# Differential attention's last batch beside the experts, and its q and k weights folded into one matrix

## The chip, the cores and the metric

The kernel runs on one core of a Trainium2 chip. The metric is the device time of one execution in microseconds. Three runs of the kernel before took 1086.4 to 1087.47 us, median 1086.97. A separate execution was taken with the hardware profiler; all profile lines below come from that one. TensorE is called PE here, VectorE DVE, ScalarE ACT, GpSimd POOL and SyncE SP. All data are float32.

## What is computed

The program is two transformer blocks on an input of 8 batches x 512 tokens x 128 channels. Block 0 adds, to x, a 16-head causal attention (head size 8) and a soft mixture of experts, both of the normalised x. Block 1 adds two things to the new x:

```python
# differential attention, per batch of 512 tokens, no mask, D = 128
q1, q2 = split(xn @ w_q12);  k1, k2 = split(xn @ w_k12);  v = xn @ w_v
diff = softmax(q1 @ k1.T * D**-0.25) - lam * softmax(q2 @ k2.T * D**-0.25)
out  = diff @ v;  out / rms(out) * 0.2

# a layer norm, a causal attention over the batch axis (8 positions), a projection, a second norm,
# then a top-2 router over 8 experts with 1280 slots each
exp_out = gelu(tokens_of_expert @ moe_w1[e]) @ moe_w2[e]
moe[token] += exp_out * prob            # each token appears in two experts
```

Since the score is `xn Wq Wk^T xn^T`, the product `Wq Wk^T` of the two weights is a 128 x 128 matrix that does not depend on the tokens.

## The kernel before, in words

The kernel has four stages, and the change is in the last two.

Stages 1 and 2 (to about 717 us) are block 0 and most of a side chain called *leads*. `l1_load` (L149) loads block 1's weights and `l1_fold` (L177) prepares them, early in stage 1, between two pieces of PE work that go in the order in which they are written. There is one lead for each of the 8 batches: the generator `lead` (L665). It runs block 1's norm, the attention over the batch axis (POOL multiplies, L722 and L751, one product a batch position; DVE sums them, through the helper at L616), the projection, the second norm and the routing, and ends with eight *puts* (L896): indirect DMAs on POOL's queue, 128 rows each, which scatter the tokens into the experts' slots `xs` in DRAM. A lead needs its batch's output of block 0, so the leads of batches 5, 6 and 7 are unfinished when stage 2 ends.

Stage 3 is the *joint stage*. The generator `diff` (L1327) does differential attention for eight batches. For a batch, `diff_qk` (L1243) makes q1, k1, q2, k2, each with a 128x512 matmul and an ACT eviction; `diff_v` makes v; then, for each of four row blocks, `diff_scores` makes two 128x512 score matmuls (L1270), a DVE maximum (L1274) and an ACT exponential (L1275); `diff_both` subtracts the two softmaxes on DVE; `diff_T` transposes; `diff_out` multiplies with v (L1304) and squares on ACT (L1308); after the last row block four small POOL instructions make the scale `ri` (L1313 to L1316), and `diff_end` (L1318) adds the result to `x_all` on DVE and stores the batch as the output's base rows (L1370). The loop at L1377 takes one step of `diff` and then lets `step_leads` (L1162) take at most one step of each unfinished lead. The turn in which a lead may go on depends on what it waits for, and one POOL step is allowed in a turn. `in_order` (L230) then fixes this order on PE, DVE, ACT and POOL.

Stage 4 is the *experts* (L1391). An expert's 1280 slots are loaded with one DMA (`xe`, L1393, after all 64 puts), in three blocks of 4, 4 and 2 tiles of 128 rows. A block is transposed and scaled (L1413), multiplied up (L1421), put through Gelu on ACT (L1424), multiplied down (L1428), scaled on DVE (`es`, L1434) and added to the output rows by indirect DMAs on POOL's queue (L1439), one a tile, ten an expert, eighty in all; these are called *backs*. Two experts may hold the same token, and so an expert's backs wait until all backs of the expert before it have landed. Expert 0's backs wait for the eight base stores. The order in stage 4 is not fixed by `in_order`: the framework's scheduler interleaves it, and it may put DVE instructions of the first experts among the last ones of `diff`.

PSUM in stage 3 is held by pools `d` (3 banks, scores), `o` (2) and `t` (3); in stage 4 by `s` (2 x 2 banks), `o` (2) and `t` (2), which take the same banks over.

Of the kernel before, what the change touches and what calls it, by code (L numbers as in the profile page):

```python
# [25 lines left out]
def kernel(ctx: ExitStack, tc: tile.TileContext, a: dict, out: bass.AP):  # L26
# [122 lines left out]
    def l1_load():  # L149
        for name, key, n in (  # L150
            ("wq1", "L1_attn_w_q12", 2 * D), ("wk1", "L1_attn_w_k12", 2 * D), ("wv1", "L1_attn_w_v", D),
            ("wr", "L1_ffn_router_weight", NE),
        ):
            l1p[name] = const.tile([P, n], F32, name=name)
            nc.sync.dma_start(out=l1p[name], in_=a[key])
        cols = const.tile([P, 4], F32, name="cols")
# [20 lines left out]
    def l1_fold():  # L177
        cols, lam, wnat = l1p["cols"], l1p["lam"], l1p["wnat"]

        lprod = wkb.tile([P, 2, D], F32, name="lprod", bufs=1)  # L180
        nc.gpsimd.tensor_tensor(out=lprod, in0=lam[:, 0:4:2], in1=lam[:, 1:4:2], op=ALU.mult)
# [6 lines left out]
        l1p["nlam"] = nlam  # L188

# [445 lines left out]
    def ln_stats(name, rows):  # L635
        stt = small.tile([P, 4, 6], F32, tag="bn_st", name=f"st_{name}")
        mv = small.tile([P, 4, 2], F32, tag="bn_mv", name=f"mv_{name}")
        for k, r in enumerate(rows):
            dve.bn_stats(out=stt[:, k, :], in_=r)
            dve.bn_aggr(out=mv[:, k, :], in_=stt[:, k, :])  # L640
            yield 1, "dve"
# [23 lines left out]
    def lead(s_):  # L665
# [37 lines left out]
        yield from after("sc", s_ - 1)  # L703
        sc = wt("sc", [NI * H, NB])
# [15 lines left out]
        for t in range(n):  # L720
# [3 lines left out]
            if len(behind) > BEHIND:  # L724
                yield 1, "dve"
                sum_q(*behind.pop(0))
# [22 lines left out]
        for t in range(n):  # L749
# [8 lines left out]
            if len(behind) > BEHIND:  # L758
                yield 1, "dve"
                dve.tensor_tensor(out=at4, in0=at4, in1=behind.pop(0), op=ALU.add)  # L760
# [130 lines left out]
        yield 3, "pool"  # L891

        for i in range(NI):
            m = s_ * NI + i
            for k in range(2):
# [8 lines left out]
                yield 1, "pool"  # L904
# [4 lines left out]
    with ExitStack() as at:  # L909
# [252 lines left out]
        def step_leads(slot_, pe_free, pool_free, more):  # L1162
            room[0] = min(room[0] + more, more)
            spare[0] = min(spare[0] + more * SPARE, CAPA * more)
            for r in list(leads):
                if slot_ < r[1] or (r[2] == "pe" and not pe_free) or (r[2] == "pool" and not pool_free):
                    continue
                if r[2] == "dve" and room[0] <= 0 or r[2] == "act" and spare[0] <= 0:
                    continue
                if r[2] == "pool":  # L1170
                    pool_free = False
                nxt = next(r[0], None)
                if nxt is None:
# [52 lines left out]
    with ExitStack() as l1b:  # L1226
# [9 lines left out]
        wka = l1b.enter_context(tc.tile_pool(name="wka", bufs=2, reuse_waits="tile"))  # L1236


        ascale = D ** (-0.25)
        OUT = (1.0 - LAMBDA_INIT) * math.sqrt(D)  # L1240
        dd = {}

        def diff_qk(b):  # L1243
            for n, (w, c) in enumerate((("wq1", 0), ("wk1", 0), ("wq1", 1), ("wk1", 1))):
                pq = psum_t(f"pqk_{b}_{n}")
                nc.tensor.matmul(pq, lhsT=l1p[w][:, c * D : (c + 1) * D], rhs=xnT[:, b], start=True, stop=True)
                dd["qk", b, n] = o = wka.tile([P, T], F32, tag=f"qk1_{n}", name=f"qk1_{b}_{n}")
                nc.scalar.activation(o, pq, AF.Identity, scale=ascale if w == "wq1" else 1.0)  # L1248
                yield
# [10 lines left out]
        def diff_scores(b, i):  # L1260
# [7 lines left out]
            for k in range(2):  # L1268
                sc = psum_t(f"s1_{u}_{k}", "d")
                nc.tensor.matmul(  # L1270
                    sc, lhsT=dd["qk", b, 2 * k][:, i * P : (i + 1) * P], rhs=dd["qk", b, 2 * k + 1],
                    start=True, stop=True,
# [25 lines left out]
        def diff_out(b, i):  # L1298
            if i == 0:
                dd["po", b] = psum_o(f"po1_{b}")  # L1300
                dd["ss", b] = small.tile([P, NI], F32, tag="ss1", name=f"ss1_{b}")
            po, dT, ss = dd["po", b][:, i * D : (i + 1) * D], dd["dT", b, i], dd["ss", b]
            for c in range(NI):
                nc.tensor.matmul(  # L1304
                    po, lhsT=dT[:, c * P : (c + 1) * P], rhs=dd["v", b][:, c], start=(c == 0), stop=(c == NI - 1),
                )
            junk = wka.tile([P, D], F32, tag="sqj1", name=f"sqj1_{b}_{i}")
# [10 lines left out]
        def diff_end(b):  # L1318
            po, ri = dd["po", b], dd["ri", b]
            for i in range(NI):  # L1320
                nc.vector.scalar_tensor_tensor(
# [3 lines left out]
            store(b)  # L1325

        def diff(bs):  # L1327
# [9 lines left out]
            more = diff_qk(bs[1])  # L1337
# [34 lines left out]

        slot_ = 4 * (N3 + 4)
        tail = len(nc.cur_bb.bb.instructions)
        run = diff(range(NB))
        going = True
        while going or leads:  # L1377
            going = next(run, "end") != "end"
            for _ in range(1):
                step_leads(slot_, True, True, 9.0)  # L1380
                slot_ += 1
        in_order(tail)
# [8 lines left out]
        for e in range(NE):  # L1391
            xe = wk.tile([P, NCT, W], F32, tag="xe", name=f"xe_{e}", bufs=3)
            get = nc.sync.dma_start(out=xe, in_=xs[e * CAP : (e + 1) * CAP].rearrange("(c p) d -> p c d", p=P))  # L1393
            for name in puts:
                tc.add_manual_dep(get.ins, name, sync, reason="any token may be in this expert's slots")

            first = small.tile([P, NCT], F32, tag="first", name=f"first_{e}", bufs=2)
# [8 lines left out]
            es = wk.tile([P, NCT, D], F32, tag="es", name=f"es_{e}", bufs=4)  # L1406
            backs.append([])
            for c0 in range(0, NCT, 4):
                n = min(4, NCT - c0)
                w = n * P  # L1410
                t = transpose4(f"xeT_p{e}_{c0}", [xe[:, c0 + k, :D] for k in range(n)])
                xeT = wk.tile([P, T], F32, tag="xeT", name=f"xeT_{e}_{c0}")
                nc.vector.tensor_scalar(  # L1413
                    out=xeT[:, :w], in0=t[:, :w], scalar1=cols[:, 2:3], scalar2=cols[:, 3:4], op0=ALU.mult, op1=ALU.add
                )
                hT = wk.tile([P, NHC, T], F32, tag="hTm", name=f"hTm_{e}_{c0}")
                for hp in range(NHC // 2):
                    ph = psum_s(f"phm_{e}_{c0}_{hp}")
                    for k in range(2):
                        hc = 2 * hp + k  # L1420
                        nc.tensor.matmul(  # L1421
                            ph[:, k, :w], lhsT=w1_1[:, e, hc * P : (hc + 1) * P], rhs=xeT[:, :w], start=True, stop=True
                        )
# [62 lines left out]
```

## Time and profile before

| | |
|---|---|
| median of three runs | 1086.97 us |
| the profiled execution's own time | 1084.87 us |
| its span, first to last instruction | 1083.1 us |
| PE matmul busy / PE weight load busy | 974.5 us (90%) / 599.0 us (55%) |
| DVE / ACT / POOL busy | 664.2 (61%) / 553.0 (51%) / 565.6 (52%) us |
| joint stage, first q matmul to the end of the last put | 717.6 to 889.0 us |
| first back to last back | 918.08 to 1077.51 us |

A busy share is a mean over four stages with different limits, so it doesn't tell what ends a stage. A line of a timeline gives the start, the time, the engine, the line of the kernel, the operation, out<-in and the count; in brackets stands the idle time of that engine just before, and what ended it by the profile. Where several semaphores are waited for, the one that came last is named, and where the named engine had long been done, it was another. "issue" means that the profile shows nothing that was waited for.

### The profile page before, as it was taken

How to read it: one execution, taken by the hardware profiler on the slowest of the kernel's cores; microseconds unless marked ns; L12 is line 12 of the kernel's file. 1: busy time of each engine (PE TensorE's matmuls, PEld its weight loads, DVE VectorE, ACT ScalarE, POOL GpSimd, SP SyncE). 2: the span in 40 equal slices, each digit the busy share in tenths (PEclk: the TensorE clock that was granted, in tenths of full speed). 3: DMA queues.
4: the chain of work that ended last, by engine and by line, in shares of the span. 5: the costliest groups of instructions: out<-in, count | busy, mean ns of one | idle time of the engine just before them, and what ended most of it. 6: DMA issues, size and time to landing. Idle time of an engine off the chain costs nothing.

```text
span 1083.1 us, 18816 instructions
## 1 busy us (share of the span) xinstructions
PE 974.5 (90%) x6726; PEld 599.0 (55%) x6726; DVE 664.2 (61%) x2126; ACT 553.0 (51%) x1263; POOL 565.6 (52%) x793
## 2 busy tenths in 40 slices
PE   6889899989999999999899999978867987999992
PEld 3457556867545454454444444435545655777772
DVE  6734643277777788888778887258676654222220
ACT  3466348353467576766565656527454653222220
POOL 3201000201242527775878879775867361777776
PEclk8999999999799999999999999779988998999997
DMA  8730000000000000000000000050000013342312
GB/s 252 158 85 2 1 1 1 2 2 1 1 1 2 2 1 2 21 2 2 14 9 3 19 2 21 2 172 1 20 11 20 21 38 103 49 67 38 31 15 25
DMA packets 49310, 32.97 MB, mean 30 GB/s; under 512 B 12232, under 2 KB 44275, under 8 KB 49216
## 3 DMA queue, kind: packets, MB, share of 16 engines
q1 hardware_dynamic: 34832, 24.80, 8.6%
q0 software_dynamic: 13568, 6.70, 4.5%
q8 instruction: 53, 0.87, 0.3%
q14 instruction: 41, 0.34, 0.1%
q10 hardware_dynamic: 816, 0.26, 0.1%
HBM read 17.56 MB, written 17.07 MB: 32 GB/s over the span
## 4 chain that ended last, share of the span: by engine, by line
PE 64%; POOL 14%; DVE 11%; issue 5%; ACT 2%; DMA 2%; POOLq 0%; DVEq 0%; SPq 0%; ACTq 0%
PE se L1068 12%; PE pem L1428 7%; PE phm L1421 6%; PE po L1093 6%; POOL xs L896 4%; PE sm L1035 3%; PE lg_d L302 3%; PE pe L477 3%; PE psl L346 3%; DVE junk L1045 2%; PE pf L379 2%; PE pq L955 2%; PE lg_c L302 2%; PE ph L451 2%; PE s L1270 2%
## 5 line engine op out<-in xcount | busy, mean ns | idle before, releaser
L1045 DVE CUSTOM_DVE_ANT_0 junk<-sm,cmask 128x128 f32<-128x128 f32 (+3 forms) x512 | 249.5, 487 | 69.3 <-PE sm L1035 31.2
L1073 ACT ACTIVATE pt<-se 128x384 f32<-128x384 f32 (+1 forms) x384 | 185.4, 527 | 158.7 <-PE sm L1035 109.7
L1035 PE MATMUL sm<-kj,qT 32*128 32x256 f32 (+3 forms) x1024 | 231.6, 487 | 5.7 <-DVE mcol L1045 3.0
L1068 PE MATMUL se<-q,kj 32*128 32x128 f32 (+3 forms) x1024 | 211.3, 483 | 3.9 <-DVE mcol L1045 3.5
L1439 POOL DMA_INDIRECT out_dram<-es,to x80 | 124.0, 1551 | 46.8 <-issue 22.8
L1068 PEld LDWEIGHTS se<-q,kj 32*128 32x128 f32 x1024 | 99.3, 190 | 84.7 <-DVE mcol L1045 26.1
L1078 POOL TENSOR_SCALAR_AFFINE_SELECT pt<-pt 128x512 f32<-128x512 f32 (+1 forms) x96 | 80.1, 835 | 115.8 <-ACT pt L1073 115.6
L1035 PEld LDWEIGHTS sm<-kj,qT 32*128 32x128 f32 x1024 | 112.6, 191 | 23.8 <-DVE mcol L1045 10.1
L1093 PE MATMUL po<-pt,vpad 128*18 128x512 f32 (+3 forms) x1024 | 91.4, 454 | 12.6 <-POOL pt L1078 12.6
L1424 ACT ACTIVATE hTm<-phm 128x1024 f32<-128x1024 f32 (+1 forms) x48 | 42.2, 881 | 109.2 <-PE phm L1421 109.2
L1428 PEld LDWEIGHTS pem<-w,hTm 128*128 128x128 f32 x640 | 77.1, 192 | 16.8 <-ACT hTm L1424 12.1
L1428 PE MATMUL pem<-w,hTm 128*128 128x128 f32 x640 | 81.2, 278 | 0.5 <-ACT hTm L1424 0.2
L1275 ACT ACTIVATE ex<-s,nm 128x512 f32<-128x512 f32 x64 | 43.9, 687 | 70.3 <-DVE nm L1274 69.7
L1434 DVE TENSOR_SCALAR es<-pem,wt 128x128 f32<-128x128 f32 x80 | 22.9, 345 | 90.0 <-PE pem L1428 90.0
L1421 PE MATMUL phm<-xeT,w 128*128 128x512 f32 (+1 forms) x192 | 75.2, 523 | 2.3 <-DVE xeT L1413 2.3
L896 POOL DMA_INDIRECT xs<-l_z,sput x64 | 65.8, 1028 | 17.0 <-issue 16.0
L508 POOL TENSOR_TENSOR x_all<-x_all,bo_bc 128x512 f32<-128x512 f32 x8 | 10.2, 1275 | 119.4 <-DVE xn L266 119.4
L1270 PE MATMUL s<-qk,qk 128*128 128x512 f32 x128 | 63.9, 620 | 6.6 <-ACT qk L1248 6.4
L1093 PEld LDWEIGHTS po<-pt,vpad 128*18 128x18 f32 x1024 | 20.9, 98 | 64.1 <-POOL pt L1078 24.0
L1274 DVE TENSOR_REDUCE nm<-s 128x1 f32<-128x512 f32 x64 | 42.9, 682 | 9.0 <-PE s L1270 8.6
L1421 PEld LDWEIGHTS phm<-xeT,w 128*128 128x128 f32 x192 | 33.6, 191 | 23.1 <-issue 17.2
L722 POOL TENSOR_TENSOR l_prod<-l_qkv 128x512 f32<-128x512 f32 x36 | 45.6, 1277 | 0.6 <-DVE l_at L616 0.6
(262 smaller groups left out, 1865.4 us busy)
## 6 DMA issues: line engine op xcount, KB each, us to landing
xs<-cmask SPq DMA_DIRECT2D x1, 5280.0 KB, 23.8
xe<-xs SPq DMA_DIRECT2D x8, 660.0 KB, 4.7
x_all<-in_L_attn_x_dram SPq DMA_DIRECT2D x8, 256.0 KB, 4.6
w<-in_L_ffn_w_dram SPq DMA_DIRECT2D x1, 2048.0 KB, 8.8
w<-in_L_ffn_moe_w_dram SPq DMA_DIRECT2D x1, 2048.0 KB, 10.0
out_dram<-x_all SPq DMA_DIRECT2D x8, 256.0 KB, 2.2
out_dram<-es,to POOLq DMA_INDIRECT x80, 3.2
xs<-l_z,sput POOLq DMA_INDIRECT x64, 2.3
```

The lines of the kernel that those rows point to most:

```text
L302: nc.tensor.matmul(lg, lhsT=lhs(k), rhs=rhs, start=True, stop=True)
L896: put = nc.gpsimd.indirect_dma_start(out=xs, out_offset=bass.IndirectOffsetOnAxis(ap=sput[:, k, m : m + 1], axis=0), in_=z2[:, i], in_offs ...
L1035: nc.tensor.matmul(sc[:, o : o + w], lhsT=st["qT", b][rr, i * P : (i + 1) * P], rhs=st["k", b, j][rr, :w], start=True, stop=True,)
L1045: nc.vector.tensor_tensor_reduce(out=junk[:, :w], in0=sc[:, o : o + w], in1=cmask[:, 512 - w : 512], scale=-1.0, scalar=BIG, op0=ALU.add, ...
L1068: nc.tensor.matmul(sc[:, o : o + w], lhsT=st["k", b, j][rr, c * P : (c + 1) * P], rhs=st["q2", b, (g % G) // 2][rr, c * P : T], start=True ...
L1073: nc.scalar.activation(st["pt", g, k][:, r, :o], sc[:, :o], AF.Exp)
L1078: nc.gpsimd.affine_select(out=pt[:, :, :n, :P], in_=pt[:, :, :n, :P], pattern=[[0, 4], [0, n], [1, P]], compare_op=ALU.is_ge, fill=0.0, ba ...
L1093: nc.tensor.matmul(po[32 * r : 32 * r + 2 * PW, c * P : T], lhsT=vpads[b % 3][:, c, at_ : at_ + 2 * PW], rhs=pt[:, r, o : o + w], start=(c ...
L1270: nc.tensor.matmul(sc, lhsT=dd["qk", b, 2 * k][:, i * P : (i + 1) * P], rhs=dd["qk", b, 2 * k + 1], start=True, stop=True,)
L1421: nc.tensor.matmul(ph[:, k, :w], lhsT=w1_1[:, e, hc * P : (hc + 1) * P], rhs=xeT[:, :w], start=True, stop=True)
L1428: nc.tensor.matmul(pe[:, k * D : (k + 1) * D], lhsT=hT[:, hc, k * P : (k + 1) * P], rhs=w2_1[:, e, hc, :], start=(hc == 0), stop=(hc == NH ...
L1439: back = nc.gpsimd.indirect_dma_start(out=out_rows, out_offset=bass.IndirectOffsetOnAxis(ap=to[:, c : c + 1], axis=0), in_=es[:, c], in_of ...
```

## The change

1. `l1_fold` transposes the four 128x128 halves of the q and k weights (PE), evicts them (ACT), multiplies them in two 128x128 matmuls into `wm1` = [Wq1 Wk1^T | Wq2 Wk2^T], and scales on eviction. `diff_qk` then makes two tiles for a batch instead of four, and the scores take `xnT` itself as the moving operand.
2. Batch 7 (`LATE`) is left out of the joint stage, whose loop runs over seven batches. Its base rows are stored without differential attention.
3. The experts are written as a pipeline of 24 blocks: the first half of the next block's up matmuls, half of this block's down matmuls, the other half of the ups, the transposes of the block after next, the other half of the downs. The whole of stages 3 and 4 is now fixed by one `in_order`.
4. From block 6 on (expert 2), three steps of batch 7's `diff` are taken in each block (two after the first half, one after the second), until its twenty-odd steps are done in block 12 (expert 4). Its scores and outputs use the two-bank pool `t`; its exponentials alternate with the Gelus on ACT, which in the built program brings 12 more loads of ACT's function table. Its four small `ri` instructions stand on POOL between the backs of experts 3 and 4.
5. Batch 7's scaled result goes to the output by one accumulating DMA on POOL's queue (`late_add`, 256 KB) between the backs of experts 6 and 7. It waits for all of expert 6's backs, and expert 7's backs wait for it.
6. In `lead`, a batch's first products may start when the lead two before it is through (was: one before; its score tile has two buffers now), and puts have a kind of their own. In a turn a lead that waits to put comes last, and POOL's one step goes to another lead first.

In the built programs the loop takes 152 turns until the last lead is through before and 118 after. On PE the order is the same up to the first matmul of `diff`, but for the six matmuls of the new fold.

```diff
 def l1_fold():
+        wqk = l1p["wqk"]
+        t = transpose4("wqkT_p", [wqk[:, n, c * D : (c + 1) * D] for c in range(2) for n in range(2)])
+        wqkT = wkb.tile([P, NI, D], F32, tag="xn2", name="wqkT", bufs=3)
+        nc.scalar.copy(wqkT.rearrange("p k d -> p (k d)"), t)
+        pm = psum_t("wm1_p")
+        for c in range(2):
+            nc.tensor.matmul(
+                pm[:, c * D : (c + 1) * D], lhsT=wqkT[:, 2 * c], rhs=wqkT[:, 2 * c + 1], start=True, stop=True
+            )
+        l1p["wm"] = wm1 = const.tile([P, 2 * D], F32, name="wm1")
+        nc.scalar.activation(wm1, pm[:, : 2 * D], AF.Identity, scale=D ** (-0.25))
...
 def lead(s_):
-        yield from after("sc", s_ - 1)
-        sc = wt("sc", [NI * H, NB])
+        yield from after("sc", s_ - 2)
+        sc = wt("sc", [NI * H, NB], bufs=2)
...
-        yield 3, "pool"
+        yield 3, "put"
...
-                yield 1, "pool"
+                yield 1, "put"
...
-        def step_leads(slot_, pe_free, pool_free, more):
+        def step_leads(slot_, pe_free, pool_free, more, at_once=()):
-            for r in list(leads):
+            for r in sorted(leads, key=lambda r: bool(at_once) and r[2] == "put"):
...
         def diff_qk(b):
-            for n, (w, c) in enumerate((("wq1", 0), ("wk1", 0), ("wq1", 1), ("wk1", 1))):
...
+            for c in range(2):
+                pq = psum_t(f"pqk_{b}_{c}")
+                nc.tensor.matmul(
+                    pq, lhsT=l1p["wm"][:, c * D : (c + 1) * D], rhs=xnT[:, b], start=True, stop=True
+                )
+                dd["qk", b, c] = o = wka.tile([P, T], F32, tag=f"qk1_{c}", name=f"qk1_{b}_{c}")
+                nc.scalar.copy(o, pq)
                 yield
...
-                sc = psum_t(f"s1_{u}_{k}", "d")
+                sc = psum_t(f"s1_{u}_{k}", "d" if b not in LATE else "t")
                 nc.tensor.matmul(
-                    sc, lhsT=dd["qk", b, 2 * k][:, i * P : (i + 1) * P], rhs=dd["qk", b, 2 * k + 1],
-                    start=True, stop=True,
+                    sc, lhsT=dd["qk", b, k][:, i * P : (i + 1) * P], rhs=xnT[:, b], start=True, stop=True
                 )
...
-        run = diff(range(NB))
+        run = diff(range(LATE[0]))
...
-                step_leads(slot_, True, True, 9.0)
+                step_leads(slot_, True, True, 9.0, ('none',))
-        in_order(tail)
+        for b in LATE:
+            store(b)
...
+        def late_add(e):
+            for _ in late:
+                pass
+            new = []
+            for b in LATE:
+                add = nc.gpsimd.dma_start(
+                    out=out[b].rearrange("(i p) d -> p i d", p=P),
+                    in_=dd["po", b].rearrange("p (i d) -> p i d", i=NI), accum_op=ALU.add,
+                )
+                for name in backs[e + 1]:
+                    tc.add_manual_dep(add.ins, name, sync, reason="a row is read and written by each addition")
+                new.append(add.ins.name)
+            backs[e + 1] = new
+
+        BLOCKS = [(e, c0, min(4, NCT - c0)) for e in range(NE) for c0 in range(0, NCT, 4)]
+        AFTER = 6
...
+        expert_T(*BLOCKS[0])
+        expert_T(*BLOCKS[1])
+        expert_up(*BLOCKS[0], 0)
+        expert_up(*BLOCKS[0], 1)
+        for m, (e, c0, n) in enumerate(BLOCKS):
+            if c0 == 0 and e + 2 < NE:
+                rows_get(e + 2)
+            half = range(n // 2), range(n // 2, n)
+            for hp in range(2):
+                if m + 1 < len(BLOCKS):
+                    expert_up(*BLOCKS[m + 1], hp)
+                if hp == 1 and m + 2 < len(BLOCKS):
+                    if BLOCKS[m + 2][1] == 0:
+                        rows_in(BLOCKS[m + 2][0])
+                    expert_T(*BLOCKS[m + 2])
+                expert_down(e, c0, n, half[hp])
+                late_steps(((2,1)[hp]) if m >= 6 else 0)
+            if e == AFTER and c0 + n == NCT:
+                late_add(e)
+        in_order(tail)
```

`rows_get`, `rows_in`, `expert_T`, `expert_up` and `expert_down` hold the load, the slot columns, the transposes, the up and Gelu, and the down, `es` and backs of the old loop, with the same shapes. `late_steps(n)` takes n steps of batch 7's `diff`.

## The prediction

> **What bounds it now.** I read the page first, then the busy times by stretch, then the timeline of POOL in the last stage, then the timeline around 889 us. The sum below is made against the profiled execution: span 1083.1, own time 1084.87; the median of the runs shown (1086.97) is 3.9 above that span, and I add 3.9 at the end. A difference under 0.2% can't be told from no change.
>
> Busy times of the joint stage (columns: PE, PE weight load, DVE, ACT, POOL, granted clock, DMA share, GB/s), and of two experts:
>
> ```profile
> 717.60:848.00 130.40, 106.29 (x478) 66.86 (x476) 97.85 (x209) 69.92 (x192) 87.99 (x130) 0.93 0.09 26
> 848.00:889.00 41.00, 41.00 (x212) 27.31 (x211) 26.81 (x67) 30.25 (x88) 23.69 (x46) 1.00 0.06 18
> 717.60:889.00 171.40, 147.29 (x687) 94.17 (x686) 124.66 (x274) 100.17 (x280) 111.68 (x176) 0.94 0.08 24
> 980.00:1020.00 40.00, 39.18 (x235) 29.61 (x235) 10.45 (x32) 10.57 (x12) 30.69 (x20) 1.00 0.25 32
> ```
>
> Until 848 no engine is full: the leads' chain from POOL to DVE paces all queues (PE idles 24.1 us). From 848 on PE is. In the experts the chain of waits names PE, and PE looks full, but the end is set elsewhere. Timeline, POOL's backs and the `es` that feed the last expert:
>
> ```profile
> 918.08 1.68 POOL L1439 DMA_INDIRECT out_dram<-es,to  x1 [9.89 <-DVE es L1434]
> ...
> 1053.36 1.13 DVE L1434 TENSOR_SCALAR es<-pem,wt 128x128 f32<-128x128 f32 x4 [2.36 <-PE pem L1428]
> ...
> 1057.17 1.55 POOL L1439 DMA_INDIRECT out_dram<-es,to  x1 [0.30 <-issue]
> ...
> 1060.84 1.55 POOL L1439 DMA_INDIRECT out_dram<-es,to  x1 [2.12 <-DMA out_dram<-es,to]
> 1062.69 1.55 POOL L1439 DMA_INDIRECT out_dram<-es,to  x1 [0.30 <-DVE es L1434]
> ...
> 1064.45 0.61 DVE L1434 TENSOR_SCALAR es<-pem,wt 128x128 f32<-128x128 f32 x2 [2.03 <-PE pem L1428]
> ...
> 1077.51 1.55 POOL L1439 DMA_INDIRECT out_dram<-es,to  x1 [0.30 <-issue]
> ```
>
> Backs follow each other at 1.853 us (1.55 + 0.30) and at 3.5 to 4.1 where an expert waits for the landing of the one before; there is no other gap. The last expert's rows were ready at 1053.36 and went out from 1060.84. So POOL's queue, 80 backs long, ends the kernel from 918.08 on: 20.4 us an expert, while PE needs 19.7 (its 28-matmul groups at 939.82, 979.24 and 1018.65 are 39.4 apart for two experts). What counts is when the first back starts, and whether POOL ever runs dry.
>
> Around the hand-over from stage 3 to stage 4:
>
> ```profile
> 888.04 0.97 POOL L896 DMA_INDIRECT xs<-l_z,sput  x1 [0.30 <-issue]
> 890.44 3.08 SPq L1393 DMA_DIRECT2D xe<-xs  x3
> 895.09 0.17 DVE L1398 TENSOR_SCALAR first<-xe 128x10 f32<-128x10 f32 x1 [8.76 <-DMA xe<-xs]
> 896.40 1.09 PE L141 MATMUL dT_p<-ident,ex 128*128 128x128 f32 x4 [6.93 <-DVE wt L1403]
> ...
> 905.11 1.16 PE L1304 MATMUL po<-v,dT 128*128 128x128 f32 x8
> ...
> 908.22 1.12 DVE L1321 SCALAR_TENSOR_TENSOR x_all<-po,ri,x_all 128x128 f32<-128x128 f32 x4 [0.67 <-POOL ri L129]
> ```
>
> An expert's `first` stands in DVE's queue ahead of the last work of `diff` and waits there for its rows; PE idles 6.93 us.
>
> **The change, part by part.**
>
> *Fold in `l1_fold`.* Four transposes (0.55 for three now), an eviction (0.59 as other 512-wide copies), two matmuls, a second eviction, in PE's written order ahead of `wT_p` at 115. The same pattern there (transpose, evict, matmul) leaves PE idle 1.7 us before `shift_p`. I take +2.0: 0.8 of work and 1.2 of waiting. Ends 0 (nothing there is full) and +3.
>
> *Joint stage.* One batch of `diff` on PE: 8 score matmuls at 0.86 (two passes 0.43 apart), 4 q/k matmuls at 0.86, 16 small ones for the output and 4 for v at 0.215, 16 transposes at 0.11: 16.4 us. The fold takes 1.7 from each of the seven that stay. So PE loses 16.4 + 12 = 28, DVE 11.0 (8 maxima at 0.68, 4 x 1.12 in `diff_both`, 4 at 0.285), ACT 13.5 + 8.4, POOL 1.7. What is left: PE 119, DVE 114, ACT 78, POOL 110. Three engines are then equally loaded, and the leads' POOL and DVE work is all still there, in 118 turns instead of 152. Bounds: 119 (PE never idle) and 171 (the leads' chain keeps its length). Keeping PE's 24 us idle gives 143; POOL as dense as in its densest stretch now, 49.91 us in the 68.2 from 717.6, gives 150. I take 146, that is -25. That lead 7's products may start under lead 6's, and that the eight puts (1.28 each) no longer stand in one piece ahead of them, is why I believe that POOL can be that dense. Eight times in ten: 134 to 160.
>
> *Hand-over.* From the last put to the first back it is 29.1 now: 17.3 until PE's last `po` (6.93 of it idle) and 11.8 after. In the new fixed order DVE's `first` stands behind all of `diff`: 10.4 remain. But the first xeT eviction now stands behind `x_all<-po` of batch 6: po, square, `ri`, `x_all` take 3.1 (906.27 to 909.35), four column instructions and the eviction 1.4. Then six half-blocks on PE at 1.72 (four 0.43 passes), a transpose and the `es` 0.9. 10.4 + 4.5 + 11.2 = 26: -3. On SP, xe's load stands behind the store of batch 5, whose `ri` stands on POOL behind the last puts: about 3 us later than now, inside the 10.4. Batch 7's base store moves ahead to the end of its lead and lands long before the first back. Ends: -7 and +3.
>
> *Expert stage.* Batch 7 brings 14.7 us of PE (16.4 - 1.7), 12 of DVE (that has 29 idle in 40), 12 of ACT, plus twelve table loads, POOL's four `ri` instructions (1.7, in the wait at an expert's boundary) and one DMA. Stage 1 shows such loads, where Gelu and exponential alternate:
>
> ```profile
> 168.70 1.28 ACT L457 ACT_TABLE_LOAD   x1
> 169.99 3.02 ACT L457 ACTIVATE hT<-ph,b1c 128x256 f32<-128x256 f32 x8
> ...
> 173.03 1.28 ACT L306 ACT_TABLE_LOAD   x1
> 174.33 0.69 ACT L306 ACTIVATE ex_c<-lg_c,nm_c 128x512 f32<-128x512 f32 x1
> ```
>
> 1.28 each, 15.4 in all; ACT has the room (10.6 of 40 busy; 38 of the 52 us below with all of it). POOL is the question. PE's matmuls of an expert at these issue times make 18.4; I allow 18.8 for the pipelined order, so in experts 0 and 1 PE gains 2 x (20.4 - 18.8) = 3.2 on POOL. Experts 2 and 3 with the pieces cost PE 2 x 18.8 + 14.7 = 52.3, POOL 40.8: POOL runs dry for 11.5 - 3.2 = 8.3. Further, with two PSUM banks the transposes of blocks 9 and 10 each wait for a score's maximum, load and exponential (0.9 + 1.28 + 0.69, less 1.7 of PE work between): 1.2 and 1.1. Sum +10.6. Afterwards POOL is the bound again and nothing is won back. Ends: 4 (pieces fill PE's small gaps) and 24 (every load stops PE). DVE's four scale instructions wait for `ri` on POOL behind expert 3's backs, and an xeT eviction is queued behind them; with POOL dry that wait is nothing, with POOL late it only spends the lead.
>
> The Trainium skill, "ScalarE: Activation LUTs", section "What ACT_TABLE_LOAD costs", puts a switch at about 2.66 us, the 1.28 load and a drain of the same length. These rows show the next ACTIVATE 0.01 to 0.02 us behind the load; by the page the twelve switches would cost 32 us and PE's waits in experts 2 and 3 would more than double.
>
> *The added DMA.* Expert 7 waits for it as an expert waits for the one before: its landing plus 0.45. Not in the trace: an accumulating direct DMA. Rows: a back (64 KB, accumulating) lands in 3.2, the base stores (256 KB) in 2.2. If issuing grows with its 512 rows, 4 x 1.55 + 1.65 + 0.45 = 8.3; as one back, 3.7. I take 4.5, nearer to the lower, since its rows are regular. Ends 3.7 and 8.3.
>
> Sum: 1083.1 + 2.0 - 25 - 3 + 10.6 + 4.5 = 1072.2, and 3.9 on it: **1076**.
>
> The Trainium skill, "Perfetto Trace Analysis", section "Identifying the Most-Contended Engine", warns that matmul busy time says little of how full PE is and points to the weight loads. Here the rows are 39.18 and 29.61 of 40. Who believes the first would add all 14.7 to the end; by POOL's queue only what exceeds its slack is added.
>
> **Rivals.**
> - *The leads set the pace (slower).* POOL and DVE pass products back and forth, PE waits, and taking PE work out of the joint stage shortens nothing: what the change adds, +14.1, is then all that is seen: 1083.1 + 2 - 3 + 10.6 + 4.5 + 3.9 = 1101. For it: PE's 24.1 idle lie all before 848. Against it: a third of the stage's turns are gone and POOL is busy only 65%. It decides if the joint stage stays above 157 us.
> - *Experts 2 and 3 are held by ACT's round trip.* Score, maximum, load, exponential, load, Gelu: the dry time is 24 instead of 10.6: 1089.5, no change or a little slower. For it: loads stand between every exponential and Gelu. Against it: the downs of the block before lie between an up and its use.
> - *More is gained.* Joint stage 134, dry time 4: 1057.5.
> - *The fold or the moving does nothing:* it can't be, the order of the built program shows both; the question is only what else is waited for.
>
> **How the numbers follow.** The forecast (joint stage 138 to 156, dry time under 18; own range 1064 to 1086) gets 0.50, the leads' pace 0.17, ACT's round trip 0.18, the larger gain 0.15. Faster: nearly all of the forecast, the larger gain and a quarter of the round trip, 0.68. Same, 0.08: a third of the round trip and the forecast's edge. Slower 0.24. Below 1055 I leave 0.07, above 1097 0.12: the range is 1055 to 1097.
>
> **What would show it.** Right: the first `pqk` to the end of the last put takes about 146 us; last put to first back 26; backs follow at 1.85 and 3.7 but for about 10 us of waits for `es` in experts 2 to 4; expert 7's first back comes 8 us after expert 6's last; twelve loads of 1.28; `wT_p` 2 us later. Wrong: a joint stage near 160, POOL idle within experts 4 to 7, PE idle over 20 us in experts 2 and 3, or an added DMA of 8 us or more.

## The result, and the profile after

The changed kernel takes 1081.6 us in the median of eight runs (1079.28 to 1082.98), the kernel before 1087.19 beside it. The ratio is 0.9955, 95% interval 0.9945 to 0.9965: faster by 0.45%, where 1.0% was forecast. In the profiled executions the span went from 1083.1 to 1079.2 us. It divides at four points that both timelines show:

| | before | after | change | forecast |
|---|---|---|---|---|
| start to first `pqk` | 714.1 | 715.3 | +1.2 | +2.0 |
| joint stage: first `pqk` to end of last put | 174.9 | 156.4 | -18.5 | -25 |
| last put to first back | 29.1 | 26.0 | -3.1 | -3 |
| first back to last back | 159.4 | 175.8 | +16.4 | +15.1 |
| last back to end | 5.6 | 5.7 | +0.1 | 0 |
| sum | | | -3.9 | -10.9 |

All but the joint stage came out within 1.3 us. The median lies 2.4 us above the profiled span, not 3.9 as assumed, and this gave back 1.5 of the 7.0 us that were missed.

Joint stage of the changed kernel by stretches, and the stages behind it (columns: PE, PE weight load, DVE, ACT, POOL, granted clock, DMA share, GB/s):

```profile
715.30:806.00 90.70, 69.96 (x293) 44.27 (x294) 78.53 (x143) 41.95 (x115) 67.00 (x89) 0.85 0.13 39
806.00:871.70 65.70, 58.70 (x294) 38.47 (x293) 49.33 (x115) 39.72 (x122) 46.59 (x87) 0.95 0.09 25
715.30:871.70 156.40, 128.66 (x586) 82.74 (x587) 127.86 (x257) 81.67 (x237) 113.58 (x175) 0.89 0.11 33
```

The same stretch of the kernel before:

```profile
714.10:889.00 174.90, 150.77 (x690) 95.68 (x691) 125.74 (x275) 100.76 (x281) 114.86 (x179) 0.93 0.10 31
```

PE lost 22 us and ACT 19, but DVE, with 18 instructions fewer, has 2 us more. In the first 90.7 us DVE is busy for 78.5, PE for 70. So DVE's instructions got longer. (The granted clock fell too, from 0.93 to 0.89. It was 0.91 with the one-input `cc` below; no run changes the clock alone, so a share of its own is not ruled out.) Groups of DVE's instructions in this stage by shape, after (busy us, mean ns; then idle time before):

```profile
L1304 DVE SCALAR_TENSOR_TENSOR ex<-ex,cc 128x512 f32<-128x512 f32 x27 | 24.6, 912 | 1.0
L630 DVE TENSOR_TENSOR l_at<-l_at,l_prod 128x512 f32<-128x512 f32 x15 | 18.2, 1212 | 2.1 <-POOL l_prod L765 2.1
L1301 DVE SCALAR_TENSOR_TENSOR cc<-sm,nlam,cc 128x1 f32<-128x1 f32 x27 | 15.6, 577 | 1.0
L630 DVE TENSOR_REDUCE l_sc<-l_prod 128x64 f32<-128x512 f32 x15 | 10.0, 670 | 0.0
```

and before:

```profile
L1288 DVE SCALAR_TENSOR_TENSOR ex<-ex,cc 128x512 f32<-128x512 f32 x29 | 23.7, 818 | 1.0
L616 DVE TENSOR_TENSOR l_at<-l_at,l_prod 128x512 f32<-128x512 f32 x15 | 16.9, 1127 | 9.2 <-POOL l_prod L751 8.9
L616 DVE TENSOR_REDUCE l_sc<-l_prod 128x64 f32<-128x512 f32 x15 | 10.1, 671 | 5.9 <-POOL l_prod L722 5.9
L1285 DVE SCALAR_TENSOR_TENSOR cc<-sm,nlam,cc 128x1 f32<-128x1 f32 x29 | 8.2, 284 | 1.0
```

`cc`, the column that subtracts the second softmax, is one number a partition, and its mean doubled; `ex` and `l_at` grew by 94 and 85 ns. These three read two tensors from SBUF. `l_sc`, a reduction of one tensor as large as theirs, did not change. The timeline of all engines at the longest `cc`:

```profile
788.12 0.97 POOL L910 DMA_INDIRECT xs<-l_z,sput  x1 [0.30 <-issue]
...
788.47 5.23 DVE L1301 SCALAR_TENSOR_TENSOR cc<-sm,nlam,cc 128x1 f32<-128x1 f32 x1
...
789.11 1.16 POOL L765 TENSOR_TENSOR l_at<-l_qkv,l_sc 128x512 f32<-128x512 f32 x1
...
790.22 1.27 POOL L804 TENSOR_TENSOR x_all<-x_all,l_ha 128x512 f32<-128x512 f32 x1
...
791.44 2.24 POOL L765 TENSOR_TENSOR l_prod<-l_qkv,l_sc 128x512 f32<-128x512 f32 x2
...
793.74 0.75 DVE L1304 SCALAR_TENSOR_TENSOR ex<-ex,cc 128x512 f32<-128x512 f32 x1
```

An instruction that takes 0.22 us as a rule begins beside the issue of a put and ends 5.23 us later, 0.02 after the last of four POOL multiplications and additions that follow each other without a gap. I call the time above the usual 0.22 (`cc`), 0.75 (`ex`) and 0.68 us (`l_at`) *holds*. They sum to 11.4 us in the joint stage before and 22.6 after (tallies differ by 0.2 with the rounding of the usual durations). A `cc` with one input, 0.27 us in the runs below, counts as not held.

The hand-over, which the kernel now has in a fixed order (timeline; SPq is SyncE's queue of DMA issues):

```profile
870.74 0.97 POOL L910 DMA_INDIRECT xs<-l_z,sput  x1 [0.31 <-issue]
...
873.14 2.97 SPq L1424 DMA_DIRECT2D xe<-xs  x3
...
878.55 1.16 PE L1322 MATMUL po<-v,dT 128*128 128x128 f32 x8 [0.52 <-ACT sqj L1328]
...
881.67 1.13 DVE L1347 SCALAR_TENSOR_TENSOR x_all<-po,ri,x_all 128x128 f32<-128x128 f32 x4 [5.30 <-POOL ri L129]
...
883.29 1.52 DVE L1447 TENSOR_SCALAR xeT<-xeT_p,cols 128x512 f32<-128x512 f32 x2
...
897.68 1.68 POOL L1486 DMA_INDIRECT out_dram<-es,to  x1 [16.05 <-DVE es L1481]
```

The last `po` ends 8.0 us behind the last put instead of 17.3, and PE no longer waits there for an expert's rows. The backs; timeline of POOL, with DVE's `es` for expert 1:

```profile
914.53 1.55 POOL L1486 DMA_INDIRECT out_dram<-es,to  x1 [0.31 <-issue]
...
916.01 1.13 DVE L1481 TENSOR_SCALAR es<-pem,wt 128x128 f32<-128x128 f32 x4 [1.24 <-PE pem L1473]
...
919.67 1.55 POOL L1486 DMA_INDIRECT out_dram<-es,to  x1 [3.58 <-issue]
...
982.10 1.55 POOL L1486 DMA_INDIRECT out_dram<-es,to  x1 [0.30 <-issue]
...
986.34 1.04 POOL L129 TENSOR_TENSOR ri<-ri,powers 128x4 f32<-128x4 f32 x1
989.53 1.64 POOL L1486 DMA_INDIRECT out_dram<-es,to  x1 [2.15 <-DVE es L1481]
...
1047.85 1.54 POOL L1486 DMA_INDIRECT out_dram<-es,to  x1 [0.30 <-issue]
1051.35 1.39 POOL L1509 DMA_DIRECT2D out_dram<-po  x1 [1.96 <-DMA out_dram<-es,to]
1056.76 1.64 POOL L1486 DMA_INDIRECT out_dram<-es,to  x1 [4.03 <-DMA out_dram<-po]
```

From 982.10 to 989.53 it is 7.43 us where expert 4 begins (3.47 before): POOL is dry, it waits for `es`. From 914.53 to 919.67, where expert 1 begins, it is 5.14 us (3.56 before), but here the rows are ready 3.3 us before the back starts. What came late is the landing of expert 0's last back, 4.3 us after its start, and the next back starts 0.83 us behind that. The added DMA puts 8.91 us between experts 6 and 7 (3.67 before).

### The profile page after: what moved, and what is told of

Its sections match the earlier page's. It is cut to its first block, busy times and chain, and to the rows that moved or that the text cites. A ratio compares the mean times of both kernels' runs of the same rounds, so it can differ in the third digit from the quotient of the medians.

```text
span 1079.2 us, 18766 instructions
## 1 busy us (share of the span) xinstructions
PE 964.9 (89%) x6702; PEld 594.3 (55%) x6702; DVE 677.6 (63%) x2130; ACT 561.3 (52%) x1261; POOL 569.0 (53%) x794
## 4 chain that ended last, share of the span: by engine, by line
PE 62%; POOL 13%; DVE 13%; issue 5%; ACT 3%; DMA 2%; POOLq 0%; SPq 0%; DVEq 0%; ACTq 0%
PE se L1082 11%; PE phm L1458 6%; PE pem L1473 6%; PE po L1107 5%; PE sm L1049 4%; PE lg_d L316 3%; PE pe L491 3%; PE psl L360 3%; DVE junk L1059 3%; PE s L1287 3%; PE pf L393 2%; POOL xs L910 2%; PE pq L969 2%; PE lg_c L316 2%; PE ph L465 2%
## 5 line engine op out<-in xcount | busy, mean ns | idle before, releaser
L1049 PEld LDWEIGHTS sm<-kj,qT 32*128 32x128 f32 x1024 | 111.4, 190 | 24.4 <-DVE mcol L1059 10.3
L1458 PE MATMUL phm<-xeT,w 128*128 128x512 f32 (+1 forms) x192 | 78.7, 534 | 4.1 <-DVE xeT L1447 3.6
L1473 PE MATMUL pem<-w,hTm 128*128 128x128 f32 x640 | 78.9, 275 | 0.0
L1287 PE MATMUL s<-xn,qk 128*128 128x512 f32 x128 | 69.4, 662 | 7.1 <-ACT qk L1265 3.9
L1447 DVE TENSOR_SCALAR xeT<-xeT_p,cols 128x512 f32<-128x512 f32 (+1 forms) x24 | 17.2, 721 | 73.9 <-PE xeT_p L141 73.9
```

Source lines behind the costliest of these rows:

```text
L1049: nc.tensor.matmul(sc[:, o : o + w], lhsT=st["qT", b][rr, i * P : (i + 1) * P], rhs=st["k", b, j][rr, :w], start=True, stop=True,)
L1287: nc.tensor.matmul(sc, lhsT=dd["qk", b, k][:, i * P : (i + 1) * P], rhs=xnT[:, b], start=True, stop=True)
L1458: nc.tensor.matmul(ph[:, k, :w], lhsT=w1_1[:, e, hc * P : (hc + 1) * P], rhs=xeT[:, :w], start=True, stop=True)
L1473: nc.tensor.matmul(pe[:, k * D : (k + 1) * D], lhsT=hT[:, hc, k * P : (k + 1) * P], rhs=w2_1[:, e, hc, :], start=(hc == 0), stop=(hc == NH ...
```

## The experiments

Two theories stood at first. *H, the holds:* POOL's multiplications hold DVE's two-tensor instructions, and that is where the joint stage's missing 6.5 us went. *L, the leads:* the order of the leads and the products handed from POOL to DVE set the stage's length, and the holds lie in spare time. A third, P, came out of the third run: while leads run their order sets the pace, afterwards PE's work does. The table has all twelve runs; the columns are us of the profiled execution, and the ratio is to the kernel before on the same chip.

| kernel | joint stage | last put to first back | first to last back | holds | ratio [95%] |
|---|---|---|---|---|---|
| before | 174.9 | 29.1 | 159.4 | 11.4 | 1 |
| changed | 156.4 | 26.0 | 175.8 | 22.6 | 0.9955 [0.9945, 0.9965] |
| changed, again | 156.5 | 26.4 | 175.8 | 22.0 | 0.9962 [0.9947, 0.9977] |
| changed, one-input `cc` | 150.0 | 27.1 | 175.5 | 15.6 | 0.9924 [0.9897, 0.9950] |
| the same, again | 150.6 | 27.6 | 175.5 | 15.7 | 0.9932 [0.9916, 0.9947] |
| before, one-input `cc` | 174.8 | 29.2 | 159.5 | 10.3 | 0.9985 [0.9968, 1.0002] |
| changed, old leads | 179.5 | 22.4 | 174.5 | 11.5 | 1.0128 [1.0097, 1.0159] |
| changed, no fold | 147.5 | 39.8 | 182.9 | 11.9 | 1.0062 [1.0040, 1.0083] |
| before, fold | 179.8 | 18.9 | 160.9 | 11.4 | 0.9967 [0.9949, 0.9986] |
| before, new leads | 144.5 | 60.5 | 159.6 | 12.4 | 1.0038 [1.0017, 1.0059] |
| before, fold and new leads | 156.2 | 43.6 | 160.6 | 22.2 | 0.9985 [0.9965, 1.0006] |
| changed, one-input `cc`, pieces spread | 153.6 | 26.9 | 172.6 | 18.5 | 0.9925 [0.9895, 0.9954] |
| the same, again | 150.5 | 27.6 | 172.8 | 15.5 | 0.9911 [0.9895, 0.9927] |
| changed, one-input `cc`, sum and product in a turn | 152.6 | 40.1 | 175.3 | 13.7 | 1.0054 [1.0037, 1.0070] |

### The column `cc` from one tensor

```diff
-            nc.vector.scalar_tensor_tensor(
-                out=cc, in0=sm[:, 0:1], scalar=l1p["nlam"], in1=cc, op0=ALU.mult, op1=ALU.mult
+            nc.vector.tensor_scalar(
+                out=cc, in0=sm[:, 0:1], scalar1=l1p["nlam"], scalar2=cc, op0=ALU.mult, op1=ALU.mult
             )
```

In the changed kernel:

> The changed kernel, with the 128x1 column cc of the differential attention made by an instruction that reads one tensor and two column scalars, where it read two tensors (27 of them in the joint stage, and 4 of batch 7 later). Theory H (holds): DVE instructions that read two tensors from SBUF don't end before the POOL TENSOR_TENSOR beside them; this time above their usual durations grew from 11.6 us before to 22.6 us after, 9.6 of it on cc (220 ns as a rule, 5230 at most), and is what the joint stage lost of its expected gain. Then cc falls to about 0.2 us each, DVE loses 9 us of busy time between the first pqk and the last put, the joint stage goes from 156.4 to 149-152 us and the time from 1081.6 to 1075-1078. Theory L (leads): the stage's length is set by the products handed from POOL to DVE and by the order of the turns; the holds lie in DVE's spare time. Then cc is short as well, but the joint stage stays at 155-157 and the time within 1.5 us of 1081.6.

In the kernel before:

> The same edit of cc in the kernel before, where cc spent only 1.9 us above its usual 0.22 us. Theory H: at most 1.5 us faster (ratio 0.9985 to 1.000), so the edit is worth several us only where POOL is denser. Theory L: no difference (1.000).

The changed kernel, its column `cc` in the joint stage as the answer for this tile gives it (duration in ns: least, median, most):

```profile
L1301 DVE SCALAR_TENSOR_TENSOR cc<-sm,nlam,cc x27: 219/220/5216, 731.7 to 873.0; 128x1 f32<-128x1 f32 x27
```

and with one tensor and two columns as inputs:

```profile
L1301 DVE TENSOR_SCALAR cc<-sm,nlam,cc x27: 272/273/276, 733.0 to 868.4; 128x1 f32<-128x1 f32 x27
```

(Both are of the second pair of runs, on one chip.) Beside the same POOL work the one-input form always takes 0.27 us. The joint stage falls from 156.4 to 150.0, as H expected; the hand-over gives 1.1 of it back, and the other parts stay. DVE's busy time there falls by 5.7 us and not by 9, since the holds on `l_at` grow by 2.8. By the ratios (0.9955 and 0.9924) the gain in time is 3.4 us, a little under the 3.6 to 6.6 of H. In the kernel before nothing is gained that can be measured.

It was repeated on one chip with the changed kernel itself, to see that the 6.5 us are not the chance of one execution:

> The changed kernel once more, beside the next three on one chip, because the length of a stage varies from execution to execution: in the runs so far the joint stage of one and the same order of work was 150.0 and 153.6 us. Theory H: the joint stage is 155 to 158 us again, with 20 to 25 us of holds on DVE, 8 to 11 of them on cc. If it comes out at 152 or less, the missing 6.5 us of the prediction were the chance of one execution, and theory H loses its ground.

> The one-input cc again. Theory H: joint stage 150 to 153.6 us as in the two runs that had it, and 3 to 6 us faster than the changed kernel beside it (ratio to it 0.994 to 0.997). Rival: within 0.1% of it.

The stage was 156.5 and 150.6 us; the medians 1082.63 and 1078.05, the ratios 0.9962 and 0.9932 with intervals that only touch. H stands in this: the holds on `cc` cost the changed kernel's joint stage some 6 us. (The four executions with the one-input `cc` and this order of work had 150.0, 150.5, 150.6 and 153.6 us.)

### The parts one by one

With the leads as they were:

```diff
-        yield from after("sc", s_ - 2)
-        sc = wt("sc", [NI * H, NB], bufs=2)
+        yield from after("sc", s_ - 1)
+        sc = wt("sc", [NI * H, NB])
...
-        yield 3, "put"
+        yield 3, "pool"
...
-                step_leads(slot_, True, True, 9.0, ('none',))
+                step_leads(slot_, True, True, 9.0)
```

> The changed kernel with the leads as before (one score tile, the next lead's products only after the one before, puts taken in the old order). The loop then takes 152 turns where it takes 135, and the last lead is done in turn 552, not 518. Theory L: the joint stage lengthens by the products' later end, to 166 or more, and the time by 10 us. Theory H: POOL is less dense, the holds fall back to about 12 us, and this wins back half: joint stage about 161, time +5. If it is not longer at all, the new order of the leads gave nothing.

Busy times of its joint stage, columns as above:

```profile
717.89:897.35 179.46, 132.85 (x628) 87.77 (x628) 121.91 (x269) 85.67 (x251) 114.39 (x183) 0.87 0.11 32
```

179.5 us, more than before the change, with PE 18 us less busy than there, idle for 47. So taking a batch and half of the q and k matmuls off PE shortens nothing in this stage by itself: L was right on this, and by more than it expected. All of the joint stage's gain hangs on the leads' new order. H's guess of half the loss was wrong, though the holds did fall to 11.5.

The fold alone (its lines of the change, put on the kernel before), and the new leads alone (the reverse of the diff above, put on the kernel before):

> The kernel before with the fold of the q and k weights alone: eight batches in the joint stage, old experts. PE loses 8 x 1.7 = 13.6 us there. If PE's idle time stays as it is (as in the prediction), the joint stage loses 13.6, the fold adds 1.2: time -12 (ratio 0.989). Theory L: only the part after the last product on POOL gains (51.5 us of PE in it, 3.1 batches x 1.7 = 5.3), time -4 (ratio 0.996).

> The kernel before with the new order of the leads alone (two score tiles, products under the lead two before, puts after other POOL steps): eight batches, four q and k tiles, old experts. The last lead is done in turn 518 as in the changed kernel, and 52 turns of PE work follow it instead of 18. Theory P (formed on the run with the old leads): while leads run, their order sets the pace, and only after them PE. The last put then ends at 870 to 877 as in the changed kernel (889.0 before), but PE's last po, 17 us behind the put before, comes 35 to 45 us behind it: about where it was (906), and the first back at 912 to 920: time 1081 to 1089, ratio 0.995 to 1.002. If instead PE's work sets the pace throughout, the last put doesn't move by more than 3 us.

The fold gave 3 us, not 12 (L had said 4): the leads end no sooner, and only PE's work behind the last put shrinks (29.1 to 18.9 us, while the last put itself comes 5 later). With the new leads the last put ends 30 us sooner in the stage, but 60.5 us of `diff` and first ups then stand behind it, and the first back comes at the same distance from the first `pqk` as before, 205.0 against 204.0. That is P's reading, though its numbers were not met: the last put came at 862.4 where 870 to 877 was expected, and the ratio, 1.0038, lies above the expected 0.995 to 1.002.

Both together (the label speaks of `cc`, but `cc` is as it was), and the changed kernel without the fold:

> The kernel before with the fold and the new order of the leads (cc as it was, batch 7 in the joint stage, old experts with no pieces and no added DMA). Theory P: last put near 872 as in the changed kernel; behind it remain 36 turns of the joint stage instead of 17, PE's last po at about 890 to 897, first back 12 us later at 902 to 909 (897.7 in the changed kernel), then 160 us of backs as before: span 1068 to 1075, time 1071 to 1078, faster than the changed kernel. If moving batch 7 is what pays, it stays above 1081.

> The changed kernel without the fold (four q and k tiles for a batch). Theory P: before the last lead product nothing changes, behind it (62 us, 58.7 of them PE, some 4 batches at 1.7) 6.8 us are added, batch 7's pieces add 1.7, the fold's own 1.2 go: +7.3, time 1089 (ratio 1.0025). If PE's work counts in the whole joint stage: 7 x 1.7 = 12 and the same rest: +12.5, time 1094 (ratio 1.007).

Measured from the first `pqk` to the first back (the first two columns): before 204.0, fold 198.7, new leads 205.0, fold and new leads 199.8, batch 7 moved with new leads 187.3, batch 7 moved and fold with old leads 201.8, all three 182.4. Ahead of the first back, moving batch 7 pays only behind the new leads, and the new leads only with batch 7 moved. P expected 187 to 194 for fold and new leads (902 to 909 less 715.3) and was wrong by 6 or more. But most of what the move wins there, 17.4 us, the experts pay back: first to last back takes 175.8 us where it took 160.6. The rest is some 2 us, and the ratio with fold and new leads, 0.9985, has an interval that overlaps that of the changed kernel's second run. Nor does the joint stage itself gain by the move: it is 156.2 us with batch 7 in it and 156.4 without; the gain lies between the last put and the first back, 43.6 and 26.0. The kernels with batch 7 moved also have the experts rewritten in a fixed order; no run has that alone, so its share is open.

P failed without the fold too. It said that nothing changes before the last product of the leads, and the joint stage went from 156.4 to 147.5. The ratio, 1.0062, was nearer to the branch in which PE's work counts everywhere (1.007), but not for its reason. Ahead of the first back it is 4.9 us; 7.1 more come in the experts, where 1.7 was expected. Pauses of 5.8 us stand within expert 4, where the changed kernel has none. As batch 7 has two more steps there, its `ri` comes on POOL behind four backs of expert 4 and not ahead of them. DVE waits for it, and an `xeT` eviction that PE needs is queued behind; timeline:

```profile
1006.13 0.88 DVE L1329 TENSOR_SCALAR po<-po,ri 128x128 f32<-128x128 f32 x4 [5.01 <-POOL ri L129]
...
1008.74 3.75 PE L1445 MATMUL phm<-xeT,w 128*128 128x512 f32 x4 [4.86 <-DVE xeT L1434]
```

The prediction had named this wait and put it at nothing; in the changed kernel it is. The ups' group from 895 us on without the fold (last column: idle before):

```profile
L1445 PE MATMUL phm<-xeT,w 128*128 128x512 f32 (+1 forms) x187 | 76.7, 533 | 6.1 <-DVE xeT L1434 4.9 <-ACT hTm L1448 0.7
```

and in the changed kernel:

```profile
L1458 PE MATMUL phm<-xeT,w 128*128 128x512 f32 (+1 forms) x176 | 69.5, 517 | 0.5
```

The column of holds suggests why the fold gave only 4.9 of its 12 us ahead of the first back. With the new leads it is 11.9 and 12.4 without the fold, 22.6 and 22.2 with it. In the same 118 turns the fold lets 27 row blocks of `diff` pass DVE where 22 passed (the count of `cc`), beside the same POOL work. This is not shown: the added row blocks bring DVE about as much work of their own (its busy time less the holds went from 94.5 to 105.3 us), and no kernel without the fold was run with the new leads and the one-input `cc`. Nor do the holds follow POOL's density alone. POOL was busy for 110.69 of 144.52 us with the new leads alone, a share of 0.77 at 12.4 us of holds; in the changed kernel it was 0.73 at 22.6. What else it takes for a `cc` to be held is open.

### Batch 7's pieces spread

```diff
-                late_steps(((2,1)[hp]) if m >= 6 else 0)
+                late_steps((1 if hp else m % 4 == 0) if m >= 1 else 0)
```

> The changed kernel with the one-input cc, and batch 7's steps spread over experts 0 to 5 (one a block, two in every fourth, from block 1) where they stood three a block from block 6. PE's surplus over POOL is then 1.6 us in each of seven experts, 11.2 against 14.7 of pieces: dry time of POOL 3.5 to 6 us where it was 11.1; four more table loads (16 for 12), which ACT has room for. First to last back 175.5 in the run with the one-input cc alone, here 168.5 to 171; time 4 to 7 us below that run's 1077.5. Rival (ACT's round trip): each piece stops PE at a score, however they are spread, and the backs' stage stays at 174 to 177.

> The spread pieces with the one-input cc again: first to last back 172 to 173.5, some 3 us below the kernel with the one-input cc alone, on one chip with it; ratio to the changed kernel 0.991 to 0.995.

First to last back: 172.6 and 172.8, against 175.5. That is 2.8 us gained of an expected 4.5 to 7; the rival, no gain, is out, but the waits for `es` were not all removed. The first of the two had a joint stage of 153.6 us and a later first `pqk` (721.4 against 715.0), so its time showed nothing. In time the step from 0.9932 to 0.9911 is within the intervals; it is the stage that shows the gain. On one chip the three medians are 1082.63 (changed), 1078.05 (one-input `cc`) and 1075.2 us (with spread pieces). The last, 0.9911 of the kernel before, interval 0.9895 to 0.9927, beats both kernels.

### A sum and the next product in one turn

```diff
-                step_leads(slot_, True, True, 9.0, ('none',))
+                step_leads(slot_, True, True, 9.0, ('sum',))
```

> The one-input cc, and a lead that has just been let do a sum on DVE may go on to its next product in the same turn: the last lead is done in turn 507, not 518 (107 turns, not 118), and 28 turns of the joint stage follow it, not 17. If turns are what sets the pace (1.25 us each while leads run), the last put ends 12 to 14 us sooner, and as 11 more turns of PE work follow, the first back comes 0 to 4 us sooner. If POOL, at 1.25 us a product, or the holds (denser POOL) set it, the first back comes no sooner, or up to 4 us later.

The joint stage with 107 turns, columns as above:

```profile
715.58:868.21 152.63, 117.31 (x510) 74.69 (x511) 109.90 (x231) 72.80 (x206) 110.39 (x171) 0.87 0.11 33
```

Eleven turns fewer, and the last put comes no sooner (152.6 against 150.6 us). PE did 9.5 us less in this time, which then stands behind the last put, and the kernel is slower by 13.6 us in the median. So it is not the count of turns that sets the pace any more. POOL is busy only 110 of the 153 us, and the holds are fewer, so neither explains it by its sum; which link of the leads' chain it is stays open.

## Why the prediction was right or wrong

**What bounds it: right.** POOL's queue of backs ends the kernel, and a later start is paid in full. With the one-input `cc` on one chip the first back came 4.7 us sooner (182.9 to 178.2 from the first `pqk`) and the median fell by 4.6.

**The fold's 2.0 us: right as far as it can be told.** On PE `shift_p` starts at 119.22, 117.23 before. It varies from execution to execution: 117.2 to 119.0 in the four without the fold, 117.8 to 121.0 in the ten with it, the medians 1.9 apart. What of it arrives at the first `pqk` can't be told: one and the same program had that point at 713.7 and 717.9 in two executions.

**The joint stage: the step that failed, "I take 146, that is -25".** It was -18.5. The 146 were counted from 717.6, 3.5 us behind the first `pqk` (which starts at 714.1, though the table of the profile before puts the first q matmul at 717.6); by the table's measure -25 means 149.9, and 156.4 came. The term of the sum that was wrong is the one that lets DVE lose 11.0 us, "So PE loses 28, DVE 11.0". DVE's own work did fall by 9.0, but its holds, which the prediction put at nothing without a reason, grew by 11.2, and its busy time rose from 125.7 to 127.9. With `cc` freed the stage takes 150.0 and 150.6 us, so the holds on `cc` are worth 6 of the 6.5 us that were missed.

That the forecast length then comes out is partly luck, for the reason given for it was only half right. The working lets PE's lost 28 us shorten the stage. PE lost 22, and the runs show that this shortens nothing: with the old leads the stage is 179.5 us, and with the new ones it is as long with batch 7 in it (156.2) as without. The prediction named the leads' new order as what lets POOL be dense, but gave it no price; alone it takes the stage from 174.9 to 144.5 us. Of the two values that the 146 lies between, the one from POOL's density came nearly true in its premise, a busy share of 0.73 in both, and it gave the longer stage (153.7 by the table's measure).

The row that could have warned was in the trace before. Its timeline at the start of the joint stage:

```profile
716.98 3.68 POOL L722 TENSOR_TENSOR l_prod<-l_qkv 128x512 f32<-128x512 f32 x3
...
717.08 4.14 DVE L616 TENSOR_TENSOR l_at<-l_at,l_prod 128x512 f32<-128x512 f32 x1 [2.42 <-POOL l_prod L751]
721.26 0.69 DVE L616 TENSOR_TENSOR l_at<-l_at,l_mx 128x512 f32<-128x512 f32 x1
721.30 1.77 POOL L722 TENSOR_TENSOR l_prod<-l_qkv 128x512 f32<-128x512 f32 x1 [0.64 <-DVE l_at L616]
```

Two-tensor instructions of one size take 4.14 us beside three multiplications of POOL, the first of which began before it, and 0.69 where the VectorE instruction began first; there POOL's multiplication takes 1.77 us, the three before it 1.23 each. The Trainium skill, "SBUF — State Buffer", section "Who interferes with whom", says that a VectorE instruction with two inputs in SBUF contends with a GpSimd instruction that reads SBUF, that the one that comes second is blocked for the whole of the other, and that an instruction with at most one such input, outside the two-port modes, is not concerned. The runs agree: 5.23 us for the two-tensor `cc`, never over 0.276 for the one-tensor form. They add that the blocked instruction is not served between two POOL instructions that follow each other closely: the long `cc` sat through four of them. Whether the put's issue held it as well no run tells.

**The hand-over: 26.0 as worked out, by two errors that cancel.** The sum was 10.4 to PE's last `po`, 4.5 to the end of the first `xeT` eviction and 11.2 to the first back. It was 8.0, 4.4 and 13.6, and 8.0, 4.4 and 14.0 in the second run. The experts' first work took longer than six half-blocks of 1.72 us, and the rest of `diff` behind the last put was shorter.

**POOL dry for 10.6 us: about 11 lost, but only 7.3 of them in the way that was forecast.** Experts 3 and 4 began 3.4 and 4.0 us late, each 0.28 us after their first rows were ready; that is POOL dry, where 10.6 was expected. The other 3.3 us stand at experts 1, 2 and 5, which began 1.6, 0.6 and 1.1 us late with their rows ready 3.3, 3.7 and 2.7 us before. There a landing of the expert before came late: 4.3, 5.0 and 3.9 us after the start of its back (at expert 2 the last back but one), where it was 2.7 for the last back ahead of experts 4, 6 and 7. The sum has no such term, so the number is right by luck. What made the landings slow was not tested. The twelve loads took 1.28 us each:

```profile
L1291 ACT ACT_TABLE_LOAD x6 | 7.7, 1283 | 2.8 <-DVE nm L1290 2.8
...
L1461 ACT ACT_TABLE_LOAD x6 | 7.7, 1283 | 0.2
```

The next ACTIVATE came 0.01 us behind all but one of them, so the dearer switch that the prediction cites did not show. The rival that ACT's round trip holds the experts fell: 24 us of dry time did not come.

**The added DMA: 4.5 forecast, 5.2 measured** (8.91 less 3.67), 1.39 of it on POOL and 4.03 waiting for its landing.

**The rival that ended slower** said that taking PE's work out shortens nothing as long as the leads set the pace, and that it decides from a joint stage of 157 us (160.5 by the table's measure). For the leads' old order that is what happens, and the change would have cost 1.3%. The new order, which the rival left out, moved the stage below that point.

## What to carry to other kernels

When work is packed more densely, list the VectorE instructions that read two SBUF tensors and stand beside GpSimd's elementwise work, and compare their mean with their shortest time: here the holds doubled, and not in step with GpSimd's density alone. One that only needs a column can take it as a scalar operand instead. A stage set by a chain between engines is not shortened by unloading the busiest engine; try the chain's order alone and the unloading alone, and expect that each may be worth nothing without the other. Where a queue bounds a stage, fill the surplus of each unit evenly with extra work, not in one block; here that gave 2.8 us.

## What the runs showed of the hardware that was not expected

- A 128x1 VectorE instruction with two tensor inputs was held for up to 5.23 us by POOL's tensor instructions; with one tensor and two column scalars it took 0.272 to 0.276 us in all 27 cases. Alone, the two-tensor form is the shorter one, 0.22.
- An accumulating direct DMA of 256 KB held POOL's queue for 1.39 us, less than one indirect back of 64 KB (1.54).
- The same program reached the same point, the first `pqk`, at 713.7 and 717.9 us in two executions, while the stages behind it were equal within 0.7 us. Stages, not absolute times, should be compared between traces.
